# Gathers issued entry by entry, a ring of slots that takes over the sets' memory, and two finishes run side by side in the last three rounds

## The chip, the cores and the metric

The kernel runs on one core of a Trainium2 chip. The metric is device time in microseconds (us) of one execution, the median of three runs. The engines are named as the profile names them: PE (matrix products), PEld (its weight loads), DVE (vector work), ACT (scalar engine), POOL (here almost only the issuer of indirect DMAs) and SP (issuer of plain DMAs).

## The reference, cut to what matters

A batch of 16 graphs ("entries") has 1024 nodes with 64 features each and a dense 1024x1024 weighted adjacency. Four layers run over each entry, every one a residual and a layer norm:

- layer 0: messages `adj @ x`, two small linear maps with a tanh;
- layer 1: messages with the adjacency divided by its row sums;
- layers 2 and 3: the adjacency is thinned by rank ("dilated"), each node takes three quantiles (0.25, 0.5, 0.75, interpolated, weighted 0.25, 0.5, 0.25) of its remaining neighbours' features, feature by feature, and the sum goes through a two-layer MLP.

```
vals = where(nd[..., None], x[:, None, :, :], inf)
s = sort(vals, axis=2)
...
agg = agg + w * (v_lo + frac * (v_hi - v_lo))
...
y = relu((x + agg) @ W1 + b1) @ W2 + b2
```

The input has about 16 neighbours a node, so the sort is of short lists. Layers 2 and 3 use the same lists of neighbours, layer 3 on the features that layer 2 put out.

## The kernel before, in words

**Preparing an entry.** `features` (L422) does layers 0 and 1 and writes the result to a table in HBM (`table[0]`, L495). `lists` (L502) thins the adjacency and makes, node by node, the list of neighbours. It uses two large buffers of the pool `sets`, tagged `near` and `takes` (the latter also holds `order`), 16 KB a partition each. Nodes are ordered by their number of neighbours, so that the 1024 rows fall into 8 tiles of 128 with lists of known greatest length: `SIZES` = 10, 11, 13, 14, 15, 17, 19 slots for the first seven tiles (t = 0 to 6), and 21 and 33 for the two halves of the last.

**Rounds.** The quantiles are done for two entries at a time. A round k is one layer (called 0 for the reference's layer 2, and 1 for its layer 3) of one pair of entries; there are 16, in the order `order_of_rounds` (L953): (0,0), (0,1), (1,0), (0,2), (1,1), ... (1,5), (0,7), (1,6), (1,7). So round 12 is layer 1 of entries 10 and 11, round 13 layer 0 of entries 14 and 15, round 14 layer 1 of entries 12 and 13, and round 15 layer 1 of entries 14 and 15. Layer 1 of a pair reads `table[1]`, which layer 0 of the pair wrote.

**A round, step by step** (`sort_round`, L1022). For each of the seven tiles, t = 6 down to 0, a task: the neighbours' rows lie in slots of `got_s`, a row of 64 numbers a slot, both entries side by side. Slot 0 is the node's own row, copied by ACT (L997). Each other slot is filled by one indirect DMA from the table, issued by POOL (`gather`, L378; 2944 in all, 184 a round). DVE sorts the slots by a fixed network of minima and maxima (`exchange`, L1014, all recorded at L211). ACT multiplies with the weights of the quantiles and DVE adds (`weigh`, L811). For the last tile the rows do not come by DMA: DVE and ACT write one-hot matrices (`hot`), PE picks rows with them (L374), and ACT copies them to `got` (`fill`, L762). Its two halves are sorted last in a round ("the tails").

**Finish.** `finish` (L848) takes the sums of one entry through the MLP and the layer norm (PE, ACT and DVE, in short steps), and POOL writes 8 tiles of rows by indirect DMA (L888): to the output in layer 1, or in layer 0 to `table[1]` from the tile `x3s`. After layer 0, `read_back` (L897) loads the table again with SP (L902) and ACT and DVE split it into three bf16 parts for the picks (`split`, L407: ACT at L410, DVE subtraction, ACT at L414, DVE, ACT). `finish_round` (L1002) runs the finish of entry m=0 to its end and then that of m=1, in every round but the last, where both run at once, the second with buffers of its own (`spare`).

**What sets the order.** DVE, ACT and PE execute in the order in which the Python code records instructions (`manual_schedule`, L1065). `Weave` (L908) mixes the generators: each `yield n` says after how many us of recorded DVE work (an estimate, `Metered`) the next step is due. POOL's and SP's instructions are ordered by the tile framework. Each engine's queue is worked in order; waits are on semaphores.

**Fetching.** `fetch` (L977) is called after each sorting instruction. It goes through the tasks in order. A task is taken when its entries (both, except in round 0) are there and its slots are free: the slots are a ring of `ROOM` = 60, and a whole round needs 99. Free means that `weigh` of the task that held the slot has been recorded. Then it records the ACT copies and all the gathers of the task.

Of the kernel before, what the change touches and what calls it, by code (L numbers as in the profile page):

```python
# [12 lines left out]
F32 = mybir.dt.float32  # L13
# [8 lines left out]
P = 128  # L22
# [3 lines left out]
SIZES = (10, 11, 13, 14, 15, 17, 19, 21, 33)  # L26
# [3 lines left out]
LINKS = [sum(SIZES[:t]) - t for t in range(LISTED + 1)]  # L30
KW = max(SIZES)
WIDE = max(2 * max(SIZES[:LISTED]), KW)
TABLES = 6
HOTS = 6
ROOM = 60
# [181 lines left out]
def adj_resnorm_kernel(ctx: ExitStack, tc: tile.TileContext, x, adj_t, nodemask, w01, b01, w02, b02,  # L217
                       w21, b21, w22, b22, w31, b31, w32, b32, out):
    nc = tc.nc
    B, N, C = x.shape  # L220
    NT = N // P
# [5 lines left out]
    s = SimpleNamespace()  # L227
# [94 lines left out]
    for t, want in enumerate(wants):  # L322
        for first, m, stride, length in regular_runs(want):
            for r in range(m):
                k = first + r * stride
# [26 lines left out]
    table = [[dram.tile([N + 1, C], F32, name=f"table{layer}{i}") for i in range(TABLES)] for layer in range(2)]  # L352
# [24 lines left out]
    def gather(dst, tab, rows):  # L377
        nc.gpsimd.indirect_dma_start(out=dst, out_offset=None, in_=tab,  # L378
                                     in_offset=bass.IndirectOffsetOnAxis(ap=rows, axis=0))
# [7 lines left out]
    def settle(dst, y, chain):  # L387

        st = s.work.tile([P, 4, NT], F32, name=f"ln_st_{chain}", bufs=1)
        dve.reduce_sum(st[:, 0], y, axis=AX.X)  # L390
        dve.tensor_scalar(st[:, 1], st[:, 0], -1.0 / C, None, op0=ALU.mult)
        yield 2
        for t in range(NT):
            nc.scalar.activation(y[:, t, :], y[:, t, :], AF.Identity, bias=st[:, 1, t : t + 1])
        nc.scalar.activation(dst, y, AF.Square)
        yield 9
        dve.reduce_sum(st[:, 2], dst, axis=AX.X)
        yield 1
        nc.scalar.activation(st[:, 3], st[:, 2], AF.Sqrt, bias=eps, scale=1.0 / C)
        yield 6  # L400
        dve.reciprocal(st[:, 0], st[:, 3])
        yield 1
        for t in range(NT):
            nc.scalar.activation(dst[:, t, :], y[:, t, :], AF.Copy, scale=st[:, 0, t : t + 1])  # L404
        yield 7
# [442 lines left out]
    def finish(b, e, layer, agg, spare=False):  # L848

        xc = e.xs[layer]  # L850
        w1s, b1c, w2s, b2r = mlps[layer]
        own, wide = ("y_x", "node_in") if spare else ("y_m", "o_t")

        def bank(name):
            if spare:
                return s.psum.tile([P, N], F32, name=name, tag="big", bufs=2)[:, :HALF]
            return s.psum.tile([P, HALF], F32, name=name, tag="m", bufs=1)

        y = s.work.tile([P, NT, C], F32, name="y_m", tag=own, bufs=1)
        dve.tensor_add(agg, agg, xc)  # L860
        yield 2
        for h in range(NH):
            pt = bank("pt")
            for q in range(G):
                nc.tensor.transpose(pt[:C, q * P : (q + 1) * P], agg[:, h * G + q, :], ident)
            yield 7
            o_t = s.work.tile([C, HALF], F32, name="o_t", tag=wide, bufs=1)
            nc.scalar.copy(o_t, pt[:C])
            yield 3
            ph = bank("ph")  # L870
            nc.tensor.matmul(ph[:H], w1s, o_t, start=True, stop=True)
            yield 7
            h_t = s.work.tile([H, HALF], F32, name="h_t", tag=wide, bufs=1)
            nc.scalar.activation(h_t, ph[:H], AF.Relu, bias=b1c)
            yield 3
            pd = bank("pd")[:, : G * C].rearrange("p (g c) -> p g c", c=C)
            for q in range(G):
                nc.tensor.matmul(pd[:, q, :], h_t[:, q * P : (q + 1) * P], w2s, start=True, stop=True)
            yield 9
            dve.tensor_add(y[:, h * G : (h + 1) * G], pd, b2r[:, None, :].to_broadcast([P, G, C]))  # L880
        dve.tensor_mul(y, y, e.mask[:, :, None].to_broadcast([P, NT, C]))
        dve.tensor_add(y, y, xc)
        xn = agg if layer else s.feat.tile([P, NT, C], F32, name="x3s", bufs=4)
        yield from settle(xn, y, "x" if spare else "m")
        yield 1
        dst, rows = (out_rows_of, e.out_rows) if layer else (table[1][b % TABLES], e.rows)
        for t in range(NT):
            put = nc.gpsimd.indirect_dma_start(  # L888
                out=dst, out_offset=bass.IndirectOffsetOnAxis(ap=rows[:, t : t + 1], axis=0), in_=xn[:, t, :],
                in_offset=None)  # L890
            tc.declare_no_dep(put.ins, group=f"rows{layer}{b}", reason="they write different rows")
            tc.add_to_no_dep_group(f"rows{layer}{b}", put.ins)
        if layer == 0:
            e.xs[1] = xn
            weave.add(read_back(b, e, dst))

    def read_back(b, e, src):  # L897

        while b >= 2 and not entries[b - 2].filled[1]:
            yield 2  # L900
        x3 = s.feat.tile([P, NT, C], F32, name="x3", bufs=1)
        nc.sync.dma_start(x3, src[:N, :].rearrange("(t p) c -> p t c", p=P))  # L902
        yield 60
        parts = s.feat.tile([P, NT, 3, C], BF, name="x3p", bufs=2)
        yield from split(x3, parts, x3)
        e.parts[1] = parts
# [41 lines left out]
                               wts=None, parts=[None, None], xs=[None, None], filled=[False, False], ends=None) for _ in range(B)]  # L948
    weave = Weave()
    tails = {}  # L950
    free, gots, room, holders = set(), [], [0], [None] * ROOM
    allowed = [1]
    order_of_rounds = [(0, 0), (0, 1)]  # L953
    for pair in range(2, B // 2):
        order_of_rounds += [(1, pair - 2), (0, pair)]
# [1 line left out]
    tasks = []  # L957
# [15 lines left out]
    def ready(b):  # L973

        return entries[b].listed and entries[b].xs[0] is not None

    def fetch(must=-1):  # L977

        while len(gots) < len(tasks):
            n = len(gots)  # L980
            k, t, present = tasks[n]
            layer, both = members(k)
            first = room[0] if room[0] + SIZES[t] <= ROOM else 0
            taken = [i for i in holders[first : first + SIZES[t]] if i is not None and tasks[i] not in free]
            there = [e.xs[1] is not None if layer else ready(b) for m, b, e in both if m in present]
            if n > must and (taken or not all(there)):
                return
            assert not taken
            holders[first : first + SIZES[t]] = [n] * SIZES[t]
            room[0] = first + SIZES[t]  # L990
            got = ring[:, :, first : first + SIZES[t], :]
            for m, b, e in both:
                if m not in present:
                    continue
                while not (e.xs[1] is not None if layer else ready(b)):
                    weave.advance()
                nc.scalar.copy(got[:, m, 0, :], e.xs[layer][:, t, :])  # L997
                for i in range(1, SIZES[t]):
                    gather(got[:, m, i, :], table[layer][b % TABLES], e.idx[:, LINKS[t] + i - 1 : LINKS[t] + i])
            gots.append(got)  # L1000

    def finish_round(k, agg, sums):  # L1002
        for gen in sums:
            while weave.runs(gen):
                yield 1
        layer, both = members(k)
        if k == len(order_of_rounds) - 1:
            for m, b, e in both:
                weave.add(finish(b, e, layer, agg[:, m], m == 1))
            return  # L1010
        for m, b, e in both:
            yield from finish(b, e, layer, agg[:, m])

    def exchange(t, pair, view):  # L1014

# [42 lines left out]
    with ExitStack() as main:  # L1058
        s.feat = main.enter_context(tc.tile_pool(name="feat", bufs=2))
        s.work = main.enter_context(tc.tile_pool(name="work", bufs=2))  # L1060
        s.sets = main.enter_context(tc.tile_pool(name="sets", bufs=1))
        s.lists = main.enter_context(tc.tile_pool(name="lists", bufs=1))
        s.psum = main.enter_context(tc.tile_pool(name="psum", bufs=1, space=bass.MemoryType.PSUM))
        engines = mybir.EngineType
        main.enter_context(tc.manual_schedule(engines={engines.DVE, engines.Activation, engines.PE}))  # L1065
        weave.add(prepare())
        rounds = []
        picked = s.psum.tile([P, 8, C], F32, name="pgk", bufs=1)
        pgs = [picked[:, :4, :], picked[:, 4:, :]]
        ring = s.lists.tile([P, 2, ROOM, C], F32, name="got_s")  # L1070
        for k in range(len(order_of_rounds)):
            allowed[0] = k + 4
            sort_round(k)
        while weave.works:
            weave.advance()
# [214 lines left out]
    with tc.If(nc.values_load(over_d[:, B:]) > 0):  # L1290
        with tc.For_i(0, B) as b:
            with tc.If(nc.values_load(over_d[:, ds(b, 1)]) > 0), ExitStack() as general:
# [6 lines left out]
                agg = s.feat.tile([P, NT, C], F32, name="agg")  # L1299
# [8 lines left out]
                with tc.tile_pool(name="g_sets", bufs=1) as s.sets:  # L1308
# [4 lines left out]
                    near = s.sets.tile([P, NT, N], BF, name="near")  # L1313
# [51 lines left out]
```

## Time and profile before

| what | value |
|---|---|
| runs | 5294.7, 5304.49, 5307.4 us; median 5304.49 us |
| the profiled execution: its own time, and its span from first to last instruction | 5293.2 us, 5291.5 us |
| busy: DVE, POOL, PE, ACT | 4296.5, 3467.3, 3412.4, 2809.6 us |
| indirect DMAs of POOL | 2944 gathers and 256 writes of rows |
| mean granted PE clock | 0.745 |

The profile has a share of busy time by engine, the same in 40 slices of 132.3 us, the groups of instructions, the waits (who waited for whom), stretches of time with each engine's busy time, and a timeline. Three things are to be kept in mind. POOL's busy time of an indirect DMA is about 1 us, and 0.30 us lie between one and the next even when nothing is waited for, shown as a wait on "issue"; so POOL is full at about 77% busy. All of DVE's instructions have one line, L211, that of the metering helper, so they are told apart by their tiles. And the chain of waits that the page prints covers only the last 22 us here (from 5269.09 us on, the output's row writes), so the stretches before it have to be read from waits and timeline.

### The profile page before, as it was taken

How to read it: one execution, taken by the hardware profiler on the slowest of the kernel's cores; microseconds unless marked ns; L12 is line 12 of the kernel's file. 1: busy time of each engine (PE TensorE's matmuls, PEld its weight loads, DVE VectorE, ACT ScalarE, POOL GpSimd, SP SyncE). 2: the span in 40 equal slices, each digit the busy share in tenths (PEclk: the TensorE clock that was granted, in tenths of full speed). 3: DMA queues.
4: the chain of work that ended last, by engine and by line, in shares of the span. 5: the costliest groups of instructions: out<-in, count | busy, mean ns of one | idle time of the engine just before them, and what ended most of it. 6: DMA issues, size and time to landing. Idle time of an engine off the chain costs nothing. (4 is left out here: it accounts for less than half of the span.)

```text
span 5291.5 us, 109614 instructions
## 1 busy us (share of the span) xinstructions
PE 3412.4 (64%) x43576; PEld 2637.1 (50%) x43576; DVE 4296.5 (81%) x9266; ACT 2809.6 (53%) x6314; POOL 3467.3 (66%) x3296
## 2 busy tenths in 40 slices
PE   6887886385765786766686775777769563424152
PEld 5656665263553665555564553655557352324141
DVE  2577848798788989897987987799899999596775
ACT  3566465466564665737383663738475653323242
POOL 0435327757477776767677674776767777777771
PEclk7888786697877787878687786877878775555555
DMA  2212212122222222221212122221212111111110
GB/s 84 79 50 72 65 39 59 46 52 53 52 54 52 59 62 57 57 57 45 70 43 57 50 48 53 57 59 50 60 51 58 25 28 26 26 24 27 26 24 7
DMA packets 420618, 259.31 MB, mean 49 GB/s; under 512 B 106603, under 2 KB 368891, under 8 KB 420091
## 3 DMA queue, kind: packets, MB, share of 16 engines
q1 hardware_dynamic: 317690, 147.12, 9.7%
q0 software_dynamic: 102400, 105.06, 9.4%
q8 instruction: 343, 5.62, 0.4%
q14 instruction: 185, 1.51, 0.1%
HBM read 239.37 MB, written 12.59 MB: 48 GB/s over the span
## 5 line engine op out<-in xcount | busy, mean ns | idle before, releaser
L378 POOL DMA_INDIRECT got_s<-table,idx x2944 | 3172.8, 1078 | 1634.3 <-issue 594.8
L374 PEld LDWEIGHTS <-hot 128*128 128x128 bf16 x24576 | 960.1, 108 | 1024.5 <-DVE hot L211 704.3
L374 PE MATMUL pgk<-x3p,hot 128*128 128x64 bf16 x12288 | 540.1, 210 | 469.6 <-DVE hot L211 402.9
L211 DVE TENSOR_TENSOR other<-got_s 128x512 f32<-128x512 f32 (+9 forms) x850 | 508.2, 609 | 390.7 <-DMA got_s<-table,idx 363.2
L374 PE MATMUL pgk<-x2p,hot 128*128 128x64 bf16 x12288 | 517.5, 207 | 321.2 <-DVE hot L211 258.9
L780 ACT COPY got<-pgk 64x256 f32<-64x256 f32 x416 | 151.9, 365 | 670.3 <-PE pgk L374 667.0
L211 DVE TENSOR_TENSOR got_s<-got_s 128x128 f32<-128x128 f32 (+9 forms) x867 | 481.9, 559 | 19.5 <-ACT got_s L829 1.7
L536 PE MATMUL pr<-steps,near 128*128 128x512 bf16 x1536 | 412.7, 429 | 131.6 <-ACT junk L542 83.5
L481 PE MATMUL pa<-x,adj_r 128*128 128x65 f32 x2048 | 387.6, 372 | 135.0 <-ACT x L404 58.1
L628 PE MATMUL pk<-near,order 128*128 128x512 f16 x2048 | 466.5, 381 | 3.9 <-DVE order L211 3.8
L829 ACT ACTIVATE got_s<-got_s,wts 128x64 f32<-128x64 f32 x1568 | 396.7, 336 | 135.4 <-DVE got_s L211 129.4
L481 PEld LDWEIGHTS pa<-x,adj_r 128*128 128x128 f32 x2048 | 377.2, 287 | 142.8 <-ACT x L404 60.1
L211 DVE TENSOR_TENSOR got_s<-other 128x512 f32<-128x512 f32 (+9 forms) x731 | 402.0, 563 | 7.5
L211 DVE TENSOR_SCALAR hot<-place 128x1024 bf16<-128x1024 f16 x768 | 329.1, 434 | 56.5 <-PE pgk L374 56.5
L211 DVE TENSOR_TENSOR other<-other 128x384 f32<-128x384 f32 (+10 forms) x617 | 323.7, 525 | 17.3
L536 PEld LDWEIGHTS <-near 128*128 128x128 f16 x1536 | 161.5, 108 | 351.8 <-issue 225.8
L211 DVE MAX8 best<-code 128x8 f16<-128x1024 f16 x240 | 293.8, 1224 | 45.9 <-ACT code L639 40.8
L628 PEld LDWEIGHTS <-order 128*128 128x128 bf16 x2048 | 193.9, 98 | 232.6 <-issue 11.6
L542 ACT ACTIVATE junk<-pr,nb_st 128x1024 f16<-128x1024 f32 x256 | 281.9, 1106 | 35.6 <-PE pr L536 34.9
L790 ACT ACTIVATE hot<-far,one_f 128x1024 bf16<-128x1024 f16 x256 | 294.0, 1148 | 8.4
L788 ACT ACTIVATE far<-place,minus_k 128x1024 f16<-128x1024 f16 x256 | 292.8, 1144 | 6.2 <-DVE place L211 4.4
L580 PE MATMUL pv<-minus_n,takes 128*128 128x128 bf16 x1024 | 209.5, 239 | 132.6 <-DVE takes L211 132.1
(205 smaller groups left out, 6727.9 us busy)
## 6 DMA issues: line engine op xcount, KB each, us to landing
adj_r<-in_adj_dram SPq DMA_DIRECT2D x256, 512.0 KB
got_s<-table,idx POOLq DMA_INDIRECT x2944
x_s<-in_x_dram SPq DMA_DIRECT2D x16, 256.0 KB
table<-x SPq DMA_DIRECT2D x16, 256.0 KB
x<-table SPq DMA_DIRECT2D x16, 256.0 KB
table<-x3s,rows POOLq DMA_INDIRECT x128
out_dram<-agg,out_rows POOLq DMA_INDIRECT x128
table<-no_row SPq DMA_DIRECT2D x12, 0.2 KB
```

Of the source, the lines that this page charges most:

```text
L211: return call(*args, **kwargs)
L374: nc.tensor.matmul(dst, hot[:, c, :], parts[:, c, q, :], start=first and c + q == 0, stop=c == NT - 1 and q == 2)
L378: nc.gpsimd.indirect_dma_start(out=dst, out_offset=None, in_=tab, in_offset=bass.IndirectOffsetOnAxis(ap=rows, axis=0))
L481: nc.tensor.matmul(pa[:, q, :], adj[i][:, jt, :], x1[:, jt, :], start=jt == 0, stop=jt == NT - 1)
L536: nc.tensor.matmul(pr[:, h * HALF : (h + 1) * HALF], near[:, c, t * P : (t + 1) * P], steps[:, ONSET + h * HALF - c * P :][:, :HALF], star ...
L542: nc.scalar.activation(junk, prs[t - 1], AF.Sign, bias=lim[:, i, t - 1 : t], scale=-1.0, accum_out=cut_at[:, i, t - 1 : t])
L580: nc.tensor.matmul(pv[:, cols], takes[:, c, rows], minus_n, start=False, stop=False)
L628: nc.tensor.matmul(cols, order[:, c, t * P : (t + 1) * P], left(c, slice(h * G, (h + 1) * G)), start=c == 0, stop=c == NT - 1)
L780: nc.scalar.copy(got[rows, off + waiting[0] : off + waiting[0] + 4, :], waiting[1][rows])
L788: nc.scalar.activation(far, e.place, AF.Abs, bias=minus_k[:, i + 2 : i + 3])
L790: nc.scalar.activation(by_act, far, AF.Relu, bias=one_f, scale=-1.0)
L829: nc.scalar.activation(got[:, m, i, :], got[:, m, slot_id, :], AF.Copy, scale=e.wts[:, t, i : i + 1])
```

## The change

`fetch` goes through the tasks for the two entries apart: m=0 may be one task ahead of m=1, and m=1 never ahead of m=0. Each takes only its own entry's readiness; m=0 allots the slots for both. Once entry 15's lists and rows are recorded (`ready(B - 1)`), the memory of the sets' tags `near` and `takes`, which no later entry needs, is taken as two further stretches of slots, 32 each, beside the 60. And the rounds from (0, 7) on, which are the last three, run their two finishes at once, the second with the spare buffers, as the last round did before.

```diff
-    free, gots, room, holders = set(), [], [0], [None] * ROOM
-    allowed = [1]
+    free, gots, room = set(), [], [0, 0]
+    allowed, fetched = [1], [0, 0]
...
     def fetch(must=-1):
 
-        while len(gots) < len(tasks):
-            n = len(gots)
-            k, t, present = tasks[n]
+        moved = True
+        while moved:
+            moved = False
+            for m in range(2):
+                n = fetched[m]
+                if n < len(tasks) and n <= fetched[1 - m] + (1, 0)[m]:
+                    moved = fetch_one(n, m, must) or moved
+
+    def fetch_one(n, m, must):
+
+        k, t, present = tasks[n]
+        if m in present:
             layer, both = members(k)
-            first = room[0] if room[0] + SIZES[t] <= ROOM else 0
-            taken = [i for i in holders[first : first + SIZES[t]] if i is not None and tasks[i] not in free]
-            there = [e.xs[1] is not None if layer else ready(b) for m, b, e in both if m in present]
-            if n > must and (taken or not all(there)):
-                return
-            assert not taken
-            holders[first : first + SIZES[t]] = [n] * SIZES[t]
-            room[0] = first + SIZES[t]
-            got = ring[:, :, first : first + SIZES[t], :]
-            for m, b, e in both:
-                if m not in present:
-                    continue
-                while not (e.xs[1] is not None if layer else ready(b)):
-                    weave.advance()
-                nc.scalar.copy(got[:, m, 0, :], e.xs[layer][:, t, :])
-                for i in range(1, SIZES[t]):
-                    gather(got[:, m, i, :], table[layer][b % TABLES], e.idx[:, LINKS[t] + i - 1 : LINKS[t] + i])
-            gots.append(got)
+            _, b, e = both[m]
+
+            def there():
+                return e.xs[1] is not None if layer else ready(b)
+
+            if n > must and not there():
+                return False
+            if n == len(gots):
+                if len(ring) == 1 and ready(B - 1):
+                    for name in ("near", "takes"):
+                        more = NT * N // (4 * C)
+                        ring.append((s.sets.tile([P, 2, more, C], F32, name="got_s", tag=name), [None] * more))
+                at, first = room
+                if first + SIZES[t] > len(ring[at][1]):
+                    at, first = (at + 1) % len(ring), 0
+                slots, holders = ring[at]
+                if any(i is not None and tasks[i] not in free for i in holders[first : first + SIZES[t]]):
+                    assert n > must
+                    return False
+                holders[first : first + SIZES[t]] = [n] * SIZES[t]
+                room[:] = at, first + SIZES[t]
+                gots.append(slots[:, :, first : first + SIZES[t], :])
+            while not there():
+                weave.advance()
+            got = gots[n]
+            nc.scalar.copy(got[:, m, 0, :], e.xs[layer][:, t, :])
+            for i in range(1, SIZES[t]):
+                gather(got[:, m, i, :], table[layer][b % TABLES], e.idx[:, LINKS[t] + i - 1 : LINKS[t] + i])
+        elif n >= len(gots):
+            return False
+        fetched[m] = n + 1
+        return True
...
         layer, both = members(k)
-        if k == len(order_of_rounds) - 1:
+        if k < order_of_rounds.index((0, B // 2 - 1)):
             for m, b, e in both:
-                weave.add(finish(b, e, layer, agg[:, m], m == 1))
-            return
-        for m, b, e in both:
-            yield from finish(b, e, layer, agg[:, m])
+                yield from finish(b, e, layer, agg[:, m])
+        else:
+            ends = [weave.add(finish(b, e, layer, agg[:, m], m == 1)) for m, b, e in both]
+            while any(weave.runs(gen) for gen in ends):
+                yield 1
...
-        ring = s.lists.tile([P, 2, ROOM, C], F32, name="got_s")
+        ring = [(s.lists.tile([P, 2, ROOM, C], F32, name="got_s"), [None] * ROOM)]
```

## The prediction, on record before the run

> **What bounds the kernel now.** I read the page's slices first, then waits and stretches of the end, then the timeline around single waits. In the slices DVE and POOL matter:
>
> ```profile
> DVE  2577848798788989897987987799899999596775
> POOL 0435327757477776767677674776767777777771
> ```
>
> POOL is full at 7 (its fixed 0.30 us between DMAs is not counted as busy). It dips to 4 to 6 now and then until slice 29, then stays at 7 from slice 30 to the last but one, while DVE falls from 9 to between 5 and 9. So DVE leads for most of the run, and POOL bounds the last 1,250 us. The stretch of that end, and the waits in it (first POOL's, then DVE's from round 13 on; columns: us in total, times, longest):
>
> ```profile
> core 0: us, PE busy (x) PEld busy (x) DVE busy (x) ACT busy (x) POOL busy (x), PEclk, DMA share, GB/s
> 3898.00:5143.00 1245.00, 615.65 (x9287) 501.21 (x9288) 1036.16 (x2148) 557.89 (x1342) 967.68 (x892) 0.65 0.14 31
> ```
> ```profile
> POOL got_s L378 <- issue: 158.2, 519, 0.3
> POOL got_s L378 <- DMA got_s<-table,idx: 56.4, 185, 0.3
> POOL got_s L378 <- DVE x L211: 20.5, 1, 20.5
> POOL got_s L378 <- DVE other L211: 12.1, 26, 2.9
> ```
> ```profile
> DVE other L211 <- DMA got_s<-table,idx: 146.7, 10, 24.9
> ```
>
> 892 DMAs in 1245 us are 1.396 us each. POOL's only real waits are the 20.5 us that end at 3897.7 and 2.9, 2.0 and 1.9 us (all others are the fixed 0.3): 7 us after the first. DVE waits 146.7 us for gathers in the last three rounds, each some 270 us long, 200 DMAs of POOL. A deeper ring cannot make a full POOL faster; it can only change which DMA goes first. The pace itself varies. While DVE stood still from 4498 to 4511, POOL issued every 1.25 us; while DVE works it takes 1.39 to 1.42 (169 DMAs in 235 us from 4180.5). I use 1.25 and 1.40.
>
> One more wait carries my forecast, the reading back of entry 13's rows (timeline: start, us, engine, line, work):
>
> ```profile
> 4437.65 1.22 POOL L888 DMA_INDIRECT table<-x3s,rows  x1 [0.30 <-issue]
> ...
> 4440.11 0.36 SPq L902 DMA_DIRECT2D x<-table  x1
> ...
> 4442.90 0.62 ACT L410 CAST x3p<-x 128x512 bf16<-128x512 f32 x1 [9.42 <-DMA x<-table]
> ...
> 4443.55 0.69 DVE L211 TENSOR_TENSOR x<-x,x3p 128x512 f32<-128x512 f32 x1 [1.74 <-ACT x3p L410]
> ```
>
> POOL's eighth row write ends at 4438.9, SP loads, ACT casts, DVE subtracts 4.7 us later. ACT had already stood 9.4 us, DVE 1.7, for POOL's turn to reach those writes.
>
> **What the Trainium skill says.** "SBUF — State Buffer", section "SBUF: two separate sides": GpSimd writes the descriptors of its DMAs itself and is locked out while DVE runs a 2-port operation. The trace agrees in direction: 1.25 us against 1.40 above. "DMA: Bandwidth & Descriptors", section "Anatomy of one DMA — SWDGE (gpsimd) path": about 2.0 us fixed, mostly the confirmation of the write. The trace has 1.7 us from the end of a gather's issue to the sort that waits for it (5132.8 to 5134.4 in round 15). "Trace analysis", titled "Perfetto Trace Analysis", section "DMA Instruction — SWDGE (GPSIMD)": the profiler's end is the end of descriptor writing, not of the transfer; so POOL's 0.94 us are issue cost, as these 1.7 us more confirm.
>
> **The change, part by part.** The order in which the changed program's instructions stand on each queue settles much; numbers of POOL are places among its 3200 indirect DMAs.
>
> *Entries apart.* Up to place 2564 (4297 us before) POOL's order is the same but for one swap of a few gathers near 1,400 us: slots, not the second entry, hold the fetch back. ACT's copies of slot 0 stand earlier, 0.3 us each, and wait for nothing. Cost 0, gain 0.
>
> *The ring grows.* It waits for PE's last reading of `near`, which ended at 4295.1; the first gather behind it is place 2588, due at 4330: no wait. Then the order differs: 196 gathers stand in a row (12 left of round 12, all 184 of round 13), and only then, at places 2760 to 2767, entry 13's eight row writes. Before, these were 2656 to 2663. They were recorded after those gathers, which now all found room. But ACT's cast and DVE's subtraction keep their places, in the middle of round 13's first task. So the read-back moves behind 104 gathers, and ACT and DVE, which work in order, stand behind it with sort, weighing, picks and finish queued.
> - DVE gets to the subtraction at 4441.8, as before (round 12 is DVE's). POOL is then at place 2666 (before: 4442.6). The 102 places to 2767 at 1.25 us, DVE standing: 127 us, to 4569; plus 4.7: 4574. Stall: 132 us.
> - In exchange the gathers of round 13 are all there. Before, the subtraction to the first tail took 184.3 us, of which 50.1 were three waits for gathers: 134.2. Tails 55.0 (4627.9 to 4682.9). Round 14 from there to the end of its t=3 task: 122.7 less a wait of 13.8, plus 4 (below): 113. Sum 302: entries 14 and 15 have their `x3s` at 4876, before 4804 and 4910.
> - Behind these stand round 15's gathers. POOL, at 1.40, comes to the first `x3s` write (place 2968) at 4569 + 200 x 1.40 = 4849 and waits 27 us. This is what reaches the end.
>
> *Finishes at once, rounds 13 and 14.* Same instructions, moved: 7 DVE steps of the second finish, about 0.57 us each, into the stretch above (4 us); its 8 row writes go ahead of most gathers of round 15 instead of among them; round 14's 16 output writes (1.3 us each) go behind the last gather, hidden under sorts until the last outputs at 5260. PE and ACT have room (half busy).
>
> *The end.* 200 places (16 writes, 184 gathers, 2968 to 3167) at 1.39, since DVE waits now and then: 278 us, from 4876 to 5154; landing 1.7, so round 15's last task starts at 5156, before 5148.9. DVE is not later: 4876, then 171.4 less waits 50.4 less 4 to round 15's start (4993), then 171.8 less waits 32.3 plus 4.5 to that task (5137), 19 us to spare. From there on before took 142.6 us; gone are the second finish's waits and steps of round 14 in it (3.0 + 2.7 + 0.9): 136. End of the span 5292, against 5291.5: +0.5. I add 2 for small waits on PE and ACT, which DVE's waits for gathers used to cover (none to 20 us). That is about 5296 beside the profiled 5293.2. The median of the runs lies 11.3 above that execution: 5307.
>
> So a large rearrangement cancels: 132 us of standing, paid back from 146.7 us of waits for gathers, since both executions issue the same DMAs through a full POOL.
>
> **The rivals.**
> - *Faster: no stall.* If the cast were not held (another order at run time is not possible, so only if I misread what its semaphore waits for), POOL would never idle: 7 us of waits gone, three DMAs fewer before the last gather (4), tail shorter by 6.6. 5304.5 - 17.6 = 5287. For: every other read-back shows no wait. Against: entry 13's did already, 9.4 us. Chance 0.14.
> - *Slower: the catching up takes longer.* Place: from the subtraction to `x3s`, 302 us with nothing hidden; each us there is a us at the end. It decides from 13 us on. Price: if POOL keeps 1.39 through the stall, 102 x 0.14 = 14; if two finishes side by side wait for PE and ACT, which the removed waits covered, up to 10 more: 24 in all, 5304.5 + 24 = 5328. For: no round before was without such cover here. Against: PE is idle half of a DVE-bound stretch (27.6 of 54 us from 4444). Chance 0.28.
> - *It does not do what it says.* The first part indeed does next to nothing; the ring does change the order. Inside the likeliest case.
>
> **How the numbers follow.** A measurement tells about 0.3% (16 us) from no change here: below 5288.6 is faster, above 5320.4 slower. Likeliest, no difference: 0.58, at 5307. The rivals lie one on each side: faster 0.14, slower 0.28. The range 5289 to 5332 takes in the slower rival and its 24 us with a little of the runs' own spread, and leaves out most of the faster one and a rest above: 2 in 10.
>
> **What would show it.** ACT at L410 and DVE's subtraction on `x` waiting some 130 us, ended by SP's load, near 4442 to 4574; no waits of DVE for gathers in rounds 13 and 14; POOL at 1.25 us in the stall; one POOL wait of about 27 us before `x3s` writes near 4876; waits for gathers only at the end of round 15. I am wrong if ACT does not stand there, if POOL stands elsewhere, or if POOL's mean per DMA differs from 1.39.

## The result, and the profile after

Five runs of each kernel give a median of 5297.45 us before (5294.7 to 5307.4) and 5335.25 us after (5328.7 to 5348.17). The ratio is 1.0069, with a 95% interval of 1.0057 to 1.0082: the change makes the kernel slower by some 38 us. The profiled execution has a span of 5326.9 us where before it was 5291.5, 35.4 more, so it shows nearly all of the loss. (The median of 5304.49 us that the prediction starts from is that of three of the five runs before.)

The slices of the two engines that mattered, on the page after:

```profile
DVE  2577848798788999897978988798999993697976
POOL 0435327757477776767677674767767777774772
```

Two new dips stand in the end. DVE falls to 3 in slice 34, which begins at 4395 us; POOL falls to 4 in slice 37, which begins at 4794 us. The stretch in which POOL issues its last gathers ends at 5191 now (before at 5143), with 888 DMAs in it:

```profile
core 0: us, PE busy (x) PEld busy (x) DVE busy (x) ACT busy (x) POOL busy (x), PEclk, DMA share, GB/s
3898.00:5191.00 1293.00, 627.55 (x9471) 511.73 (x9468) 1049.09 (x2178) 575.97 (x1386) 961.48 (x888) 0.65 0.14 30
```

POOL did nearly the same work, yet took 48 us longer. The waits say where. First those of DVE from 4411 to 5200 us, then those of POOL from 3898 to 5191 us (us in total, times, longest):

```profile
DVE x L211 <- ACT x3p L410: 136.0, 2, 132.2
DVE agg L211 <- DMA out_dram<-agg,out_rows: 34.8, 1, 34.8
DVE other L211 <- DMA got_s<-table,idx: 23.4, 3, 10.4
```
```profile
...
POOL table L888 <- ACT x3s L404: 56.4, 3, 55.8
...
POOL got_s L378 <- DVE x L211: 20.5, 1, 20.5
```

DVE's waits for gathers fell from 146.7 to 23.4 us, and a standing of 132.2 us at the read-back took their place; both were forecast. The second line was not: 34.8 us in one wait, for the output rows of round 12. It is followed by POOL's own idle time of 55.8 us, where 27 were forecast. The records of that stretch, first POOL's last output row and DVE's addition, then POOL's alone (start, us, engine, line, work, idle time before it):

```profile
4852.36 0.97 POOL L888 DMA_INDIRECT out_dram<-agg,out_rows  x1 [0.31 <-issue]
...
4854.64 0.29 DVE L211 TENSOR_TENSOR agg<-got_s 128x128 f32<-128x128 f32 x1 [34.84 <-DMA out_dram<-agg,out_rows]
```
```profile
4852.36 0.97 POOL L888 DMA_INDIRECT out_dram<-agg,out_rows  x1 [0.31 <-issue]
4909.09 1.00 POOL L888 DMA_INDIRECT table<-x3s,rows  x1 [55.76 <-ACT x3s L404]
```

The name `agg` explains it. There are two buffers for the sums, so round 14's are written where round 12's were, and round 12's may be overwritten only when its output rows have been read out of it. The second entry's eight output rows are POOL's places 2960 to 2967 now (4843.4 to 4853.3 us); before they were places 2872 to 2879 (4727.1 to 4737.9). They moved by 88 places, behind gathers that found room in the longer ring, just as the read-back's rows did. DVE's first addition into round 14's sums kept its place in DVE's order. It waits at 4819.8, and everything that DVE has behind it stands too, the two finishes that make the rows of entries 14 and 15 among it. POOL finishes its last output row at 4853.3 and has only those rows next, so it idles until 4909.1.

The kernel before had the same wait, at its smallest (DVE's record, from the timeline of before):

```profile
4739.22 0.29 DVE L211 TENSOR_TENSOR agg<-got_s 128x128 f32<-128x128 f32 x1 [5.97 <-DMA out_dram<-agg,out_rows]
```

These 6 us of waiting tell that this buffer had no slack left: whatever delays those rows by more than it delays DVE lengthens the wait.

### The profile page after: what moved, and what is told of

The parts are those of the page before. It is cut to its first block, busy times and chain, and to the rows that moved or that the text cites. A ratio compares the mean times of both kernels' runs of the same rounds, so it can differ in the third digit from the quotient of the medians.

```text
span 5326.9 us, 109567 instructions
## 1 busy us (share of the span) xinstructions
PE 3412.9 (64%) x43576; PEld 2639.3 (50%) x43576; DVE 4295.7 (81%) x9266; ACT 2809.0 (53%) x6314; POOL 3466.4 (65%) x3296
## 5 line engine op out<-in xcount | busy, mean ns | idle before, releaser
L542 ACT ACTIVATE junk<-pr,nb_st 128x1024 f16<-128x1024 f32 x256 | 281.8, 1106 | 33.8 <-PE pr L536 33.0
L450 PE MATMUL px<-adj_r,x_s 128*64 128x128 f32 x2048 | 287.3, 302 | 12.3 <-ACT node_in L453 9.0
```

The costliest lines, as they stand in the source:

```text
L450: nc.tensor.matmul(px[C:, q * P : (q + 1) * P], x_s[:, jt, :], adj[t][:, jt, :], start=jt == 0, stop=jt == NT - 1)
L542: nc.scalar.activation(junk, prs[t - 1], AF.Sign, bias=lim[:, i, t - 1 : t], scale=-1.0, accum_out=cut_at[:, i, t - 1 : t])
```

## The experiments

Four single edits were used, alone and together. "Apart" gives round 14's sums memory that nobody else uses by then:

```diff
-        agg = s.feat.tile([P, 2, NT, C], F32, name="agg")
+        spare = dict(tag="adj_r", bufs=3) if k == len(order_of_rounds) - 2 else {}
+        agg = s.feat.tile([P, 2, NT, C], F32, name="agg", **spare)
```

"Late" puts the split of entry 13's read-back off, so that DVE comes to it when it has long landed:

```diff
-        yield 60
+        yield 200 if b == B - 3 else 60
```

"No ring" leaves out the growth of the ring and keeps the rest of the change:

```diff
-                if len(ring) == 1 and ready(B - 1):
+                if False:
```

"Light" takes one bf16 part of three in the picks, so that the picked rows are rounded and 16,384 matmuls are left out; no instruction of DVE, ACT or POOL changes its place:

```diff
-            for q in range(3):
+            for q in range(1):
                 nc.tensor.matmul(dst, hot[:, c, :], parts[:, c, q, :], start=first and c + q == 0,
-                                 stop=c == NT - 1 and q == 2)
+                                 stop=c == NT - 1 and q == 0)
```

**Light kernels: before (e7) and after (e8).** In the first sets of full kernels, told further below, the kernel before itself took 7.5 ms and POOL no longer bounded its end. The light kernels were made to see that end without most of the picks' matmuls.

> The kernel before with one bf16 part of each feature in the picks instead of three (8 matmuls of a pick where there were 24): the picked rows are rounded, and 16,384 of TensorE's 43,576 matmuls are left out; every other instruction stays where it was. It is to see the end of the kernel without TensorE's slow issue of its own instructions, which bound e1 to e6. If that issue goes with the number of matmuls, DVE and POOL bound the end again, DVE waits about 147 us for gathers in the last three rounds, and the time is 5250 to 5400. If TensorE's slowness has another cause (a clock, a slower memory), it stays near 7000.

> The changed kernel with the same matmuls left out. If TensorE is out of the way: the standing of some 132 us at the read-back, the wait of some 35 us for output rows before round 14's sums, POOL idle some 56 us before the rows of entries 14 and 15, and 30 to 40 us more than the kernel before without the same matmuls. If the loss had come from two finishes sharing TensorE, it would shrink to under 10 us here.

Measured on one chip, where the full kernel before took 5298.19 us: e7 5256.8 us (5255.92 to 5260.45), ratio to the full kernel before 0.9919 [0.9902, 0.9936]; e8 5289.59 us (5286.89 to 5300.09), ratio 0.9981 [0.9973, 0.9989]. The loss is 33 us, with two thirds of the picks' matmuls gone. DVE's waits from 4370 to 5200 us in e8 and POOL's from 3898 to 5170 are those of the changed kernel (the same stretches are used for e13 to e16):

```profile
DVE x L211 <- ACT x3p L410: 133.6, 2, 132.1
DVE agg L211 <- DMA out_dram<-agg,out_rows: 36.1, 1, 36.1
```
```profile
POOL table L888 <- ACT x3s L404: 56.4, 3, 55.8
```

So the load of those matmuls is not what costs the time, and light kernels stand for the full ones in what follows. All that they show is shown for them; for the full kernels it rests on their having the same waits.

**Which wait costs it: e13, e14, e15, e16**, all on e8, in one set on one chip (full kernel before: 5309.81 us there, 5298.46 to 5319.29).

> As e8 (the changed kernel with one part of three in the picks), with round 14's sums in memory of their own. My theory (the loss is DVE's 36 us of waiting for output rows before round 14's sums): that wait is gone, the standing of 132 us stays, POOL's wait before the rows of entries 14 and 15 falls from 55.8 to about 21 us: 35 us less than e8, about 5255, equal to e7. Rival (the standing of 132 us is the loss): a wait comes up elsewhere, 5280 to 5292.

Measured: 5258.38 us (5252.13 to 5263.85), ratio 0.9899 [0.9881, 0.9917]. That is 31 us below e8 by the medians, 35 by the spans of the profiled executions (5296.8 and 5262.1) and 0.8% of the kernel before by the ratios; e8 ran on another chip. Beside e14, which ran in the same set and keeps the wait, it is 36 us less. DVE's waits and POOL's in e13's end:

```profile
DVE x L211 <- ACT x3p L410: 133.7, 2, 132.2
DVE other L211 <- DMA got_s<-table,idx: 25.9, 3, 10.4
```
```profile
POOL table L888 <- ACT x3s L404: 15.9, 3, 15.3
```

The standing of 132.2 us is still there, and the loss is gone. The line on `agg` has vanished, and POOL idles 15.3 us instead of 55.8, where about 21 were expected.

> As e8, with the split of entry 13's read-back put off to the end of round 13's last task. My theory: the standing of 132 us goes, yet DVE now stands some 120 to 150 us before round 14's sums, for the same output rows at the same places of POOL, which comes there about 13 us later without its pace beside an idle DVE: 5295 to 5310, slower than e8. Rival (the standing is the loss): 5230 to 5257.

Measured: 5294.14 us (5290.99 to 5298.81), ratio 0.9973 [0.9961, 0.9984]. Now the standing is gone, and the time is that of e8, a little under the lower end of what was expected. DVE's waits in e14, and two stretches of it:

```profile
DVE agg L211 <- DMA out_dram<-agg,out_rows: 146.3, 1, 146.3
DVE other L211 <- DMA got_s<-table,idx: 50.5, 6, 10.6
DVE x L211 <- ACT x3p L410: 5.7, 2, 4.2
```
```profile
4450.00:4665.00 215.00, 51.11 (x488) 36.18 (x489) 180.48 (x379) 83.05 (x221) 168.68 (x153) 0.51 0.13 25
4672.00:4816.00 144.00, 0.00 (x0) 0.00 (x0) 0.00 (x0) 1.32 (x2) 108.73 (x115) 0.50 0.13 26
```

DVE saved 132 us and lost 146.3 at the next wait, for rows whose place on POOL had not moved. The two stretches (columns as above: POOL is the fifth pair) fit its losing no more: POOL issues 153 DMAs in 215 us beside a working DVE, 1.405 us each, and 115 in 144 us beside a standing one, 1.252 each. The expectation had left this second gain out.

> Both edits on e8. My theory: no such wait is left and POOL never idles after 3898 us; place 3167 about 12 us earlier than in e13, where POOL still waits some 21 us but gains 13 in the standing: 5240 to 5250, 45 to 65 less than e14 and about 10 less than e7. If the sums' buffer did not matter, e15 equals e14.

Measured: 5246.41 us (5242.01 to 5249.01), ratio 0.9882 [0.9865, 0.9898]. Against e14, which differs only in the sums' buffer, this is 48 us less; against e13, which differs only in the standing, it is 12 us less. POOL's only waits for `x3s` are the fixed 0.3 us, and DVE's waits for gathers are back at 142.1 us, near the 149.1 of e7:

```profile
DVE other L211 <- DMA got_s<-table,idx: 142.1, 16, 28.6
DVE x L211 <- ACT x3p L410: 10.2, 2, 6.1
```

> As e8 without the growth of the ring (entries apart and both finishes at once stay). My theory: POOL's order is that of the kernel before up to place 2955, neither the standing nor the sums' wait comes, POOL stays full, its last gather stands three places earlier and the tail is 7 to 8 us shorter: 8 to 14 us less than e7, 5243 to 5249. Rival (two finishes at once cost by themselves): 5262 to 5290.

Measured: 5248.61 us (5246.8 to 5251.52), ratio 0.9884 [0.9868, 0.9901]. DVE's waits are those of e7, without the standing and with the wait on `agg` at its old size:

```profile
DVE other L211 <- DMA got_s<-table,idx: 141.2, 10, 23.7
DVE agg L211 <- DMA out_dram<-agg,out_rows: 6.3, 1, 6.3
```

It is 8 us below e7 by the medians, from two chips; by the ratios to the kernel before it is 0.35% below, and the two intervals hardly part. So the entries apart and the two finishes at once cost nothing where POOL bounds the end, and may be a small gain; the loss comes with the ring. It is not the ring as such: e15 has the ring and is as fast as e16. A kernel with the ring whose finishes stay one after the other was not run, so whether both finishes at once add to the loss beside the ring is not shown.

**The same edits in the full kernel: e1 to e6, e9 to e12, e17, e18.** In the four sets of these twelve runs the kernel before took 7478 to 7503 us. (In the run of the change itself, and in the sets of e7, e8 and of e13 to e16, it took some 5300.)

> Round 14's sums get memory of their own (the adjacency tiles', dead by then), all else as after the change. My theory now: the loss is the 34.8 us that DVE stands before its first addition into round 14's sums, because they share a buffer with round 12's, whose second entry's output rows moved behind round 13's and 14's gathers to POOL's places 2960 to 2967. Then this wait is gone, entries 14 and 15 have their rows some 35 us earlier, POOL's wait before them falls from 55.8 to about 21 us, and the time falls by about 35 us, to 5300, near the kernel before. Rival: the loss is the 132 us of standing at the read-back, which can't be caught up; the sums' buffer only shows where it comes out. Then DVE or POOL waits elsewhere instead, and the time stays at 5325 to 5340.

> The split of entry 13's read-back is put off to the end of round 13's last task, so that nothing stands 132 us before it; sums' buffers and the ring as after the change. My theory (the sums' buffer): the 132 us are gone, but DVE still waits for the same output rows, at the same places of POOL, now far longer than 34.8 us, and POOL has lost its faster pace during the standing (about 13 us): 5335 to 5350. Rival (the standing is the loss): faster than the changed kernel by 40 us or more, 5280 to 5295.

> Both edits: sums of round 14 apart, split of entry 13 put off. My theory: neither wait is left, POOL never idles from 3898 us on; 604 places from 2564 at 1.395 us end at 5144, then 1.7 and the 134 us of the tail: span 5280, time about 5288, 10 under the kernel before. If the rival is right that the standing is the loss, this gives the same as e2, 5280 to 5295, and e2 and e3 agree; under mine they differ by 50 us or more.

> The change without the growth of the ring: entries apart and both finishes at once stay. POOL's order is that of the kernel before up to place 2955, the second entry's output rows of round 12 at places 2872 to 2879 again. My theory: neither the standing nor the sums' wait; POOL stays full, the last gather stands three places earlier (-4 us), the tail is 7 to 8 us shorter: time 5285 to 5290, 8 to 12 under the kernel before. Rival: finishing both entries at once is itself what costs (PE and ACT shared by two finishes); then this stays slower than before, 5300 to 5335.

> Round 14's sums in memory of their own, everything else as after the change; again, since e1 to e4 ran where the kernel before itself took 7478 us[...], so that POOL was not the bound of the end. Where the kernel before takes some 5300 us: my theory (the sums' buffer) expects DVE's wait of 34.8 us for output rows gone, POOL's wait before the rows of entries 14 and 15 down from 55.8 to about 21 us, and 5300 us, near the kernel before. Rival (the 132 us of standing at the read-back are the loss): DVE or POOL waits elsewhere instead, 5325 to 5340.

> The change without the growth of the ring, again for the same reason. My theory: neither the standing at the read-back nor the sums' wait; POOL stays full from 3898 us on, the last gather stands three places earlier, the tail is 7 to 8 us shorter: 5285 to 5290 where the kernel before takes 5297. Rival (two finishes at once cost what they share on PE and ACT): 5300 to 5335.

> The changed kernel in full, with round 14's sums in memory of their own (the adjacency tiles', dead by then). For a chip on which the kernel before takes some 5300 us. My theory (the loss is DVE's 34.8 us of waiting for output rows before it may write round 14's sums, which share a buffer with round 12's): this wait is gone, the standing of 132 us stays, POOL's wait before the rows of entries 14 and 15 falls from 55.8 to about 21 us: 35 us less than the changed kernel, about the kernel before (0 to +5 us). Rival (the 132 us of standing are the loss): a wait comes up elsewhere, and 30 to 40 us over the kernel before stay.

> The changed kernel in full, with the split of entry 13's read-back put off to the end of round 13's last task. My theory: the standing of 132 us goes, yet DVE stands before round 14's sums for the same output rows at the same places of POOL, more than 100 us in place of 34.8, less what waits for gathers take back; POOL, no longer at its pace beside an idle DVE, comes there about 13 us later: +40 to +55 us over the kernel before. Rival (the standing is the loss): no slower than the kernel before, -20 to 0.

> Both edits in the full changed kernel. My theory: neither wait is left and POOL never idles from 3898 us on; places 2564 to 3167 at 1.395 us each end at 5144, then 1.7 and the tail's 134: span 5280, -10 us against the kernel before, 45 to 60 less than e10. If the standing alone mattered, e10 and e11 agree within 10 us.

> The change without the growth of the ring (entries apart, both finishes at once). My theory: POOL's order is that of the kernel before up to place 2955, neither the standing nor the sums' wait comes; POOL stays full, its last gather stands three places earlier, the tail is 7 to 8 us shorter: -8 to -14 us against the kernel before. Rival (finishing two entries at once costs by itself): +5 to +35.

> The change without the growth of the ring, all matmuls in. Where TensorE is not the bound (the kernel before at some 5300 us): as e16 against e7, 8 to 18 us less than the kernel before, so faster than both kernels. Rival (two finishes at once cost more with all the picks' matmuls beside them): 0 to +20 us. On a chip where the kernel before takes 7.5 ms: some 60 us more than it, as e4, e6 and e12.

> The changed kernel with round 14's sums in memory of their own, all matmuls in. Where TensorE is not the bound: as e13 against e7, within 10 us of the kernel before, 30 to 40 us less than the changed kernel. Rival (the wait matters only when the picks are light): 30 to 40 us over the kernel before. On a chip where the kernel before takes 7.5 ms: some 150 us more than it, as e1, e5 and e9.

Measured, as ratios to the kernel before on the same chip:

| edit on the changed kernel | ratios with their intervals |
|---|---|
| apart (e1, e5, e9, e18) | 1.0229 [1.0195, 1.0263], 1.0201 [1.0174, 1.0228], 1.0200 [1.0169, 1.0231], 1.0196 [1.0164, 1.0228] |
| late (e2, e10) | 1.0203 [1.0169, 1.0237], 1.0172 [1.0138, 1.0206] |
| apart and late (e3, e11) | 1.0218 [1.0183, 1.0253], 1.0207 [1.0175, 1.0238] |
| no ring (e4, e6, e12, e17) | 1.0116 [1.0080, 1.0152], 1.0099 [1.0077, 1.0121], 1.0072 [1.0043, 1.0100], 1.0112 [1.0079, 1.0144] |

These say nothing on the question, because something else bounds there. Apart, late and both agree within their intervals, so POOL's part of the end is hidden. TensorE's longest line of waits in e1 points to what bounds instead:

```profile
PE pgk L374 <- issue: 1060.4, 1059, 32.4
```

After the change, in the run with 5.3 ms, TensorE's waits of this kind come to 9.4 us, none of them for picks ("issue" is time in which an engine waits for nothing that the profile shows). The records of e4 show it closely:

```profile
2039.66 0.26 PE L515 MATMUL pm<-one,near 128*128 128x1 bf16 x4 [0.42 <-issue]
2040.39 0.16 PE L515 MATMUL pm<-one,near 128*128 128x1 bf16 x1 [0.48 <-issue]
2041.11 0.26 PE L515 MATMUL pm<-one,near 128*128 128x1 bf16 x4 [0.56 <-issue]
2042.55 0.26 PE L515 MATMUL pm<-one,near 128*128 128x1 bf16 x4 [1.18 <-issue]
```

TensorE waits for nothing that the profile shows, and still starts only one or a few matmuls every 0.72 us or twice that. There the change without the ring costs about 1%, and with the ring and one or both of the other edits about 2%, for reasons that these runs don't settle. The changed kernel itself was not run there, and no full variant where the kernel before takes 5300 us. So that e15's or e16's edit beats both kernels is shown for light kernels, and for full ones it is only likely.

## Why the prediction was wrong

The prediction gave 5307 us, in a range of 5289 to 5332; the median was 5335.25. Most of its chain held, step by step:

- *The ring moves the read-back.* Held. DVE stood 132.2 us (forecast 132), from 4446.3 to 4578.4 (4442 to 4574), ACT 139.9 us at L410, and SP's load ended it:

```profile
4574.67 0.36 SPq L902 DMA_DIRECT2D x<-table  x1
...
4577.78 0.62 ACT L410 CAST x3p<-x 128x512 bf16<-128x512 f32 x1 [139.90 <-DMA x<-table]
...
4578.43 0.69 DVE L211 TENSOR_TENSOR x<-x,x3p 128x512 f32<-128x512 f32 x1 [132.18 <-ACT x3p L410]
```

- *POOL beside a standing DVE.* Held. 105 DMAs in the 130 us from 4447 are 1.238 us each (forecast 1.25), and 169 in the 240 us from 4580 are 1.420:

```profile
4447.00:4577.00 130.00, 0.77 (x15) 0.61 (x12) 0.00 (x0) 0.00 (x0) 98.31 (x105) 0.50 0.15 28
4580.00:4820.00 240.00, 116.77 (x1833) 98.28 (x1834) 227.16 (x472) 108.19 (x275) 188.56 (x169) 0.59 0.13 24
```

- *The waits for gathers go.* Held. None is left in rounds 13 and 14; three remain in round 15, the last of them ended by the last gather, 23.4 us together.
- *Entries 14 and 15 have their rows at 4876.* This failed. POOL wrote the first at 4909.1, 33 us later.
- *200 places at 1.39.* Nearly: from 4909.1 to 5190.9 they took 281.8 us, 1.409 each, 4 us more than the forecast 278.
- *The tail.* From the last gather's issue to the end 136.0 us, where 1.7 of landing and 136 were forecast: 2 less.

33 and 4 less 2 are the 35 us between the forecast end of 5292 and the span of 5326.9. The forecast for the median was off by only 28 us, because it had 2 us of margin in it and because the median lay 6.6 us above the profiled execution, not the 11.3 carried over from the runs before; the latter was luck.

The step that failed is the sum behind 4876: "Round 14 from there to the end of its t=3 task: 122.7 less a wait of 13.8, plus 4 (below): 113". The 122.7 us are taken from the kernel before, and 6.0 of them are the wait on `agg`, which this sum carried along as if it were work of a fixed length. It is a wait for POOL. The prediction's own numbers would have priced it: DVE comes to that addition at 4574 + 134.2 + 55.0 + 50.4 (from round 14's start at 4682.9 to where the wait began before, at 4733.3) = 4813.6; POOL ends place 2967 where it was said to reach 2968, at 4849, and DVE went on 1.3 us after the last row's issue. That is a wait of 36.7, against 34.8 measured; put in for the 6.0, it moves the rows of entries 14 and 15 from 4876 to 4907, beside 4909.1 measured. In the list of DVE's waits from which the forecast took its first row, the 146.7 us for gathers, this wait was the second row.

That the loss is this wait is shown, on the light kernels, by e13 and e14: without it the loss is gone though the standing remains, and without the standing the loss remains. The prediction's claim that the 132 us are paid back from waits for gathers is shown as well: e13, which still has them, ends beside e7 (ratios 0.9899 and 0.9919, with overlapping intervals). They don't cancel to nothing, though: e15 is 12 us under e13. From place 2564 on, e13 gains 12.9 us by its standing (to place 2767 in 271.9 us, e15 in 284.7); then e15 gains 3.4 us to place 2967, 15.0 us of POOL's idle time, and 6.1 us from place 2968 to 3167 (275.9 us against 282.0), where its DVE waits more for gathers. The balance is 11.6 us for e15; the profiled spans differ by 21.8, and the other 10 lie before place 2564, where the two edits change nothing.

Of the rivals, the slower one had the place right, between the subtraction and `x3s` with nothing hidden, where each us is a us at the end. Its mechanism was wrong: PE's load was not the cause, since e8 loses 33 us with most of the picks' matmuls gone; in e13 both finishes still run at once, with all that they ask of PE and ACT, and the loss is gone; and POOL did take its faster pace. (The reading set against this rival, PE idle for 27.6 of 54 us from 4444, was wrong: the view of that stretch has PE busy for 34.95 us, so it idles for 19.) The faster rival fell with the 132.2 us.

## What to carry to other kernels

A deeper prefetch ring on a full queue changes only who goes first, so list what else that queue carries: each write that slides behind the new prefetches delays whoever needs its data and whoever needs the buffer that it reads. A wait of a few us for a buffer's release is a sign that its slack is used up; follow it through the change even when it is the smallest line, and never carry a wait along inside a duration taken from the old trace. And two waits one after the other for the same queue can overlap: taking away the first, as in e14, only lengthened the second.

## What was not expected of the hardware

POOL was faster in both places where DVE stands: 1.238 us a DMA in the changed kernel and 1.252 in e14, against 1.405 to 1.420 beside a working DVE. In e14 the standing came later, and the faster pace with it. This had been read off before, yet e14's expectation missed that its longer wait brings the pace back. No run shows which of DVE's instructions slow POOL.

In some sets of runs the same kernel took 7.5 ms instead of 5.3. Over the span, DVE's busy time was the same (4308.2 us in e1, 4295.7 after the change), but TensorE started its instructions in steps of about 0.72 us for long stretches, with no wait that the profile shows. It is not settled by the chip's number alone: e9 to e12 and e13 to e16 are both on record with chip 0, and the kernel before took 7503 us in the first of these sets and 5310 in the second. All four sets of experiments with full variants had these times, the kernel before too; the two sets with light ones and the run of the change itself, which had full kernels only, did not. So the cause stays open.
